# Loading half of the first memory features first, and moving their transposes and three copies, in the head of a gated cross attention kernel

## The chip, the cores and the metric

The kernel runs on one core of a Trainium2 chip. Its metric is the device time of one execution in microseconds (us). All data are float32. The engines are called as the profile calls them: PE is TensorE (with PEld, its weight loads), DVE is VectorE, ACT is ScalarE, POOL is GpSimd, and SP issues most of the DMAs. SBUF is the on-chip memory of 128 partitions, PSUM the accumulators that PE writes.

## The reference

It is cross attention to a short memory, with a gate and a norm. Batch 8, 1024 tokens of 1024 features, 64 memory rows of 512 features for each batch entry:

```python
memory_proj = einsum('bme,de->bmd', memory, W_mem)               # (8, 64, 1024)
scores = einsum('bnd,bmd->bnm', hidden_states, memory_proj) / sqrt(D)
attn = softmax(scores, axis=-1)
memory_context = einsum('bnm,bmd->bnd', attn, memory_proj)
gate_input = concatenate([hidden_states, memory_context], axis=-1)
gate = sigmoid(einsum('bnf,df->bnd', gate_input, W_gate) + b_gate)
fused = hidden_states + gate * memory_context
return fused * rsqrt(mean(square(fused), axis=-1) + 1e-6) * norm_w
```

The host hands the kernel W_mem and W_gate transposed, so that their rows are features of the input.

## The kernel before, in words

The main loop takes the 8192 tokens in 16 groups of 512. The large product (tokens by the upper half of W_gate) is made by two nested levels of a scheme with seven products in the place of eight; sums of operands run on DVE and POOL, sums of results mostly on DVE. Ahead of the loop stands a setup of some 80 us: the projected memory (products `pm1` to `pm7`), then its product with the lower half of W_gate (`mg1` to `mg7`, rows `pg` of the profile), and the sums of the W_gate blocks that the loop uses. This change touches only the first microseconds of that setup, the head.

All instructions of the head are pinned: each engine runs its own in the order in which the program writes them, and each waits by semaphores for what it reads or overwrites. There is no planner at work there.

The head, in the order of the program. Line numbers are those of the profile of before.

1. `zeros` is cleared (L115), and PE runs four warm-up matmuls `pz` on it. A float32 matmul shows as two records in the profile, a transpose as one.
2. SP issues the loads (L98), 512 KB each: the first half of the memory (`memq[0]`: 256 of the 512 memory rows, two to a partition, with all 512 features), chunks 0 and 1 of W_mem (`wm[:, k]`, a chunk being 128 input features by 1024 outputs), the second half of the memory (`memq[1]`), chunks 2 and 3. The eight chunks `w2` of the lower half of W_gate, two loads of 2 MB of the upper half (`w1`) and the norm's weights follow at once on the same queue.
3. `transpose_mem(0)` (L193): PE turns the first half of the memory, one 128x128 block at a time. For each chunk k of 128 features it makes two transposes into the PSUM tile `pt[k]`, and a copy (L200) brings the result into `memT` in SBUF. Even k is copied by DVE, odd k by ACT. `memT[0]` holds k = 0 and 1, `memT[1]` holds k = 2 and 3.
4. The products read halves of W_mem's columns that lie interleaved; some are copied first into dense tiles. `pw[:, 0]` is such a copy of chunk 1 (POOL, L284), `pw[:, 1]` of chunk 2 (ACT, L285), `pw_b[:, 0]` of chunk 3 (ACT, L290), `pw22` of the other halves of chunks 2 and 3 (ACT, L298).
5. Product 1 (`p1`): its first half takes chunk 0 straight from `wm` and k = 0 of `memT`, its second half `pw[:, 0]` and k = 1. Each half is 8 matmul records.
6. DVE makes `ps1` in two halves, sums of chunk 0 with chunk 2, and of chunk 1 with chunk 3 (L95, `pm_s<-wm` 128x512).
7. `transpose_mem(1)` does the same for the second half of the memory; here k = 0, 1 are copied by ACT, k = 2, 3 by DVE. It writes other columns of the same four PSUM tiles.
8. ACT copies product 1's result to `pu` (L293).
9. Product 2 reads the columns of `memT[1]` (k = 2, 3) that belong to the first half of the memory: first half `pw[:, 1]`, second half `pw_b[:, 0]`, 8 records each.
10. DVE makes `pt1`, `ps2`, `pt2`; product 5 needs `ps1` and `pt1`, product 6 `ps2` and `pt2`. DVE adds product 2 to `pu` and goes on with `ps3` and `ps4`; POOL makes two sums `e12` (after `pt1`) and `e21` (after `pt2`), in place in `memT`. Product 7 needs `ps3` and `e12`, product 3 `ps4`, product 4 `pw22` and `e21`. POOL then starts the sums `t1`, `t2` (rows `t_w`) of the `w2` chunks; `t2` is needed by the product `mg6`.

Of the kernel before, what the change touches and what calls it, by code (L numbers as in the profile page):

```python
# [10 lines left out]
ALU = mybir.AluOpType  # L11
# [9 lines left out]
def tile_gated_cross_attention_rmsnorm(  # L21
# [42 lines left out]
    nc = tc.nc  # L64
    B, N, D = x.shape
    M, E = mem.shape[1:]
# [5 lines left out]
    KE = E // P  # L72
# [16 lines left out]
    pin = tc.keep_in_program_order  # L89

    def mm(o, lhsT, rhs, start, stop):
        pin(nc.tensor.matmul(o, lhsT, rhs, start=start, stop=stop, skip_group_check=True))  # L92

    def tt(eng, o, a, b, op):
        pin(eng.tensor_tensor(o, a, b, op))  # L95

    def load(o, i):
        pin(nc.sync.dma_start(o, i))  # L98

    def t4k(pool, shape, tag, name):  # L100
        return pool.tile(shape, F32, tag=tag, name=name)
# [9 lines left out]
    def bank(tag, shape, name):  # L111
        return ps.tile(shape, F32, tag=tag, name=name)
# [1 line left out]
    zeros = t4k(small, [P, C], "junk", "zeros")  # L114
    pin(nc.vector.memset(zeros, 0.0))  # L115
    pz = bank("af0", [P, C], "pz")
    for _ in range(4):
        mm(pz, zeros[:, :P], zeros, True, True)


    memr = mem.rearrange("b m e -> (b m) e").rearrange("(g p s) e -> g p s e", g=2, p=P)
    memq = [t4k(rot, [P, 2, E], "l2", f"memq{i}") for i in range(2)]
    wm = t4k(xqpool, [P, KE, D], "xq", "wm")
    wmr = w_mem_t.rearrange("(k p) d -> p k d", p=P)
    load(memq[0], memr[0])
    for k in (0, 1):
        load(wm[:, k, :], wmr[:, k, :])
    load(memq[1], memr[1])
    for k in (2, 3):
        load(wm[:, k, :], wmr[:, k, :])  # L130
# [51 lines left out]
    mgd = dram.tile([2, BM, D], F32, name="mgd")  # L182
    memT = [t4k(rot, [P, 2, BM], "u", f"memT{i}") for i in range(2)]

    def transpose_mem(g):


        cols = slice(g * (BM // 2), (g + 1) * (BM // 2))
        for k in range(KE):
            for r in range(2):  # L190
                n = 2 * g + r
                pin(
                    nc.tensor.transpose(  # L193
                        pt[k][:, n * P : (n + 1) * P], memq[g][:, r, k * P : (k + 1) * P], ident
                    )
                )
            o = memT[k // 2][:, k % 2, cols]
            copy = nc.scalar.copy if (k < 2 if g else k % 2) else nc.vector.tensor_copy
            pin(
                copy(  # L200
                    o.rearrange("p (c r) -> p r c", r=2),
                    pt[k][:, cols].rearrange("p (r c) -> p r c", r=2),
                )
            )
# [33 lines left out]
    def split(t, r):  # L238

        return t.rearrange("p k (m j) -> p k j m", j=KD)[:, :, KH * r : KH * (r + 1), :]  # L240

    def pm_left(pool, tag, name):
        return t4k(pool, [P, 2, KH, P], tag, name)

    def pm_product(n, l, r, k_first=False):

        pgs = [setup_bank(f"pm{n}_{i}") for i in range(2)]
        if not isinstance(l, tuple):
            l = l[:, 0], l[:, 1]
        order = [(j, k) for j in range(KH) for k in range(2)]  # L250
        if k_first:
            order.sort(key=lambda jk: jk[1])
        for j, k in order:
            o = pgs[j // 2][:, (j % 2) * HM : (j % 2 + 1) * HM]
            mm(o, l[k][:, j, :], r[:, k, :], j % 2 == 0 and k == 0, k == 1)
        return pgs
# [7 lines left out]
    w11, w12 = (split(wm[:, 2 * k : 2 * k + 2, :], 0) for k in range(2))  # L264
    w21, w22 = (split(wm[:, 2 * k : 2 * k + 2, :], 1) for k in range(2))
# [5 lines left out]
    ps1 = pm_left(apool, "s1", "pm_s1")  # L271
# [6 lines left out]
    def pm_dense(o):  # L278
        t = const.tile([P, 3, 2, C], F32, tag=f"it{o}", name=f"pm_it{o}")[:, :2]
        return t.rearrange("p a k c -> p (a k c)").rearrange("p (k j m) -> p k j m", k=2, j=KH)  # L280

    pw22, pw, pw_b = pm_dense(1), pm_dense(2), pm_dense(3)
    transpose_mem(0)
    pin(nc.gpsimd.tensor_copy(pw[:, 0], w11[:, 1]))  # L284
    pin(nc.scalar.copy(pw[:, 1], w12[:, 0]))  # L285
    p1 = pm_product(1, (w11[:, 0], pw[:, 0]), e11, True)
    for k in range(2):
        tt(nc.vector, ps1[:, k], w21[:, k], w22[:, k], ALU.add)
    transpose_mem(1)
    pin(nc.scalar.copy(pw_b[:, 0], w12[:, 1]))  # L290
    for i in range(2):
        pin(
            nc.scalar.copy(  # L293
# [733 lines left out]
```

## Time and profile before

| | |
|---|---|
| median of 3 runs | 953.75 us (953.73, 953.75, 954.67) |
| the profiled execution | 953.63 us |
| its span, first to last instruction | 951.8 us |
| PE busy | 939.9 us, 99% of the span |
| DVE, POOL, ACT busy | 806.5, 711.0, 361.9 us |
| from PE's first matmul to the first transpose | 1.19 to 4.76 us |
| transposes of the first half of the memory | 4.76 to 6.47 us |
| product 1 | 6.47 to 10.17 us |
| transposes of the second half | 10.17 to 11.04 us |
| product 2 | 11.04 to 14.50 us |

A row of the timeline begins with its start and its length in us; then come the engine, the line, the operation, the output tile and the tiles that it is made from, shapes, and how many records it merges. The bracket at the end, where there is one, is the time for which the engine stood idle before it, and what ended that. In the digit rows of the page each digit is one fortieth of the span, some 24 us, and 9 means 90% busy or more. The chain of work that ended last is followed backwards from the last instruction, at each step to what released it. Names come without buffer numbers: `pm_it` stands for `pw`, `pw_b`, `pw22`, `pt1`, `pt2` and `ps4`, `pm_s` for `ps1` to `ps3`, `pm_t` for `pu`.

### The profile page before, as it was taken

The numbers are of one execution on the slowest core, as the hardware profiler recorded it, in microseconds if no ns is written. First come the engines' busy times: TensorE is split into PE (matmuls) and PEld (weight loads), VectorE is DVE, ScalarE is ACT, GpSimd is POOL, SyncE is SP. The second block draws the span as 40 slices with busy tenths as digits, with TensorE's granted clock in tenths as the row PEclk, the third lists the DMA queues.
The fourth block names the chain that finished last, engine by engine and source line by source line (L and its number), as shares of the span: only waits on it lengthen the run. The fifth ranks groups of instructions, "written<-read, shape, count | busy, mean of one in ns | idle before, by whom it ended". The sixth has DMA issues, their size and how long they took to land.

```text
span 951.8 us, 15584 instructions
## 1 busy us (share of the span) xinstructions
PE 939.9 (99%) x5624; PEld 732.1 (77%) x5624; DVE 806.5 (85%) x1258; ACT 361.9 (38%) x782; POOL 711.0 (75%) x780
## 2 busy tenths in 40 slices
PE   9999999999999999999999999999999999999995
PEld 8546778787877778787877778687877778787773
DVE  6988888888888888888888888888888888888887
ACT  3001235162433525153443526253443526243456
POOL 5997877688676777787686867777686767877683
PEclk9999999999999999999999999999999999999998
DMA  9956664482919365481918366391918466390632
GB/s 377 285 144 161 105 122 112 108 181 48 206 46 185 98 130 131 103 185 39 217 45 174 93 141 138 90 199 32 215 53 166 101 133 144 79 210 25 144 142 89
DMA packets 70923, 128.40 MB, mean 135 GB/s; under 512 B 12352, under 2 KB 49216, under 8 KB 70592
## 3 DMA queue, kind: packets, MB, share of 16 engines
q1 hardware_dynamic: 61664, 93.86, 37.5%
q0 software_dynamic: 9184, 33.56, 19.4%
q8 instruction: 45, 0.74, 0.3%
q14 instruction: 30, 0.25, 0.1%
HBM read 87.56 MB, written 41.68 MB: 136 GB/s over the span
## 4 chain that ended last, share of the span: by engine, by line
PE 97%; DVE 2%; ACT 1%; issue 0%; DVEq 0%
PE af L92 31%; PE ed L92 21%; PE pc L92 10%; PE kC L92 10%; PE kB L92 10%; PE pg L92 5%; PE psT_af L92 5%; PE pm L92 3%; DVE gate L95 1%; PE psT_ed L92 0%; PE pz L92 0%; DVE gate L788 0%; PE sc L430 0%; PE pa L461 0%; PE psT_b L92 0%; PE pt L193 0%
## 5 line engine op out<-in xcount | busy, mean ns | idle before, releaser
L95 POOL TENSOR_TENSOR gate<-gate,u 128x512 f32<-128x512 f32 (+1 forms) x224 | 236.9, 1070 | 187.4 <-DVE u L95 151.3
L685 ACT ACTIVATE gate<-gate 128x512 f32<-128x512 f32 x128 | 80.2, 630 | 225.0 <-DVE gate L95 225.0
L352 DVE STREAM_TRANSPOSE a<-xq 128x512 f32<-128x512 f32 x128 | 141.5, 1108 | 3.4 <-issue 3.4
L95 POOL TENSOR_TENSOR l<-a 128x256 f32<-128x256 f32 x128 | 110.9, 866 | 18.6 <-PE af L92 17.5
L714 DVE SCALAR_TENSOR_TENSOR gate<-gate,ss,nw_sb 128x512 f32<-128x512 f32 x120 | 119.4, 995 | 1.1
L92 PE MATMUL pc<-mg,attnT 64*64 64x512 f32 x512 | 116.8, 595 | 0.1
L92 PE MATMUL ed<-it,l 128*128 128x256 f32 x448 | 115.0, 379 | 0.0
L92 PE MATMUL kB<-it,l 128*128 128x256 f32 x448 | 115.0, 379 | 0.0
L95 DVE TENSOR_TENSOR gate<-gate,pc 128x512 f32<-128x512 f32 x128 | 86.1, 682 | 31.7 <-ACT gate L685 31.7
L901 ACT COPY u<-af 128x256 f32<-128x256 f32 x112 | 40.7, 363 | 182.6 <-PE af L92 182.6
L92 PE MATMUL af<-w,a 128*128 128x256 f32 x384 | 98.5, 379 | 0.0
L92 PEld LDWEIGHTS kB<-it,l 128*128 128x128 f32 x448 | 85.1, 190 | 11.6
L95 DVE TENSOR_TENSOR gate<-gate,ed 128x512 f32<-128x512 f32 x112 | 76.1, 679 | 19.1 <-POOL gate L95 17.5
L92 PEld LDWEIGHTS ed<-it,l 128*128 128x128 f32 x448 | 83.9, 190 | 10.7
L95 DVE TENSOR_TENSOR gate<-gate,af 128x512 f32<-128x512 f32 (+1 forms) x128 | 76.7, 609 | 12.8 <-PE af L92 11.2
L92 PEld LDWEIGHTS af<-w,a 128*128 128x128 f32 x384 | 73.0, 190 | 10.3 <-issue 0.5
L95 POOL TENSOR_TENSOR l<-s 128x256 f32<-128x256 f32 x96 | 78.2, 814 | 3.3 <-DVE it L95 3.3
L92 PEld LDWEIGHTS pc<-mg,attnT 64*64 64x64 f32 x512 | 32.9, 132 | 50.1 <-issue 23.5
L92 PE MATMUL af<-mg,attnT 64*64 64x256 f32 (+1 forms) x384 | 67.4, 456 | 0.0
L92 PE MATMUL ed<-it,a 128*128 128x256 f32 x256 | 67.4, 386 | 0.0
L95 DVE TENSOR_TENSOR u<-u,kC 128x256 f32<-128x256 f32 x112 | 45.9, 410 | 23.8 <-PE kC L92 20.3
L92 PE MATMUL af<-t,s 128*128 128x256 f32 x256 | 65.8, 379 | 0.0
(147 smaller groups left out, 2044.6 us busy)
## 6 DMA issues: line engine op xcount, KB each, us to landing
xq<-in_x SPq DMA_DIRECT2D x64, 512.0 KB, 10.3
gate<-in_x POOLq DMA_DIRECT2D x60, 512.0 KB, 8.4
out<-gate SPq DMA_DIRECT2D x60, 512.0 KB, 3.3
w<-in_w_gate_t SPq DMA_DIRECT2D x8, 512.0 KB, 10.2
w<-in_w_gate_t SPq DMA_DIRECT2D x2, 2048.0 KB, 17.2
mg<-mgd SPq DMA_DIRECT2D x16, 256.0 KB, 5.2
wm<-in_w_mem_t SPq DMA_DIRECT2D x4, 512.0 KB, 6.0
mpd<-mpT SPq DMA_DIRECT2D x4, 512.0 KB, 8.6
```

Source lines behind the costliest of these rows:

```text
L92: pin(nc.tensor.matmul(o, lhsT, rhs, start=start, stop=stop, skip_group_check=True))
L95: pin(eng.tensor_tensor(o, a, b, op))
L352: nc.vector.transpose(A[key][:, :, r * P : (r + 1) * P], chunks(xq[q][:, 4 * t : 4 * t + 4, :], KD)[:, half * KH : (half + 1) * KH],)
L685: pin(nc.scalar.activation(g, g, AF.Sigmoid))
L714: nc.vector.scalar_tensor_tensor(g[:, cols], g[:, cols], rstd[:, t % 2 : t % 2 + 1], nw_sb[:, cols], ALU.mult, ALU.mult,)
L901: pin(nc.scalar.copy(p1, af[:, 0]))
```

## The change

Four edits, all in the head:

- One of the four warm-up matmuls is left out.
- The first half of the memory is loaded in two pieces: features 0 to 255 (k = 0, 1) in front, features 256 to 511 (k = 2, 3) behind chunks 0 and 1 of W_mem. Each piece has 256 KB, in runs of 1 KB where the whole load had runs of 4 KB.
- Only k = 0 and 1 are transposed ahead of product 1; k = 2 and 3 are transposed behind it, just ahead of the second half of the memory. In the first half k = 0 is now copied by DVE and k = 1, 2, 3 by ACT (before: 0 and 2 by DVE, 1 and 3 by ACT).
- The copies of chunks 2 and 3 (`pw[:, 1]`, `pw_b[:, 0]`) go from ACT to POOL, which runs them behind its copy of chunk 1; that of chunk 3 keeps its place in the program behind the transposes of the second half. DVE makes the second half of `ps1` behind its two copies of the second half's transposes, no longer ahead of them.

```diff
-    for _ in range(4):
+    for _ in range(3):
         mm(pz, zeros[:, :P], zeros, True, True)
...
-    load(memq[0], memr[0])
+    load(memq[0][:, :, : E // 2], memr[0][:, :, : E // 2])
     for k in (0, 1):
         load(wm[:, k, :], wmr[:, k, :])
+    load(memq[0][:, :, E // 2 :], memr[0][:, :, E // 2 :])
     load(memq[1], memr[1])
...
-    def transpose_mem(g):
+    def transpose_mem(g, ks=range(KE)):
         cols = slice(g * (BM // 2), (g + 1) * (BM // 2))
-        for k in range(KE):
+        for k in ks:
...
-            copy = nc.scalar.copy if (k < 2 if g else k % 2) else nc.vector.tensor_copy
+            copy = nc.scalar.copy if (k < 2 if g else k) else nc.vector.tensor_copy
...
-    transpose_mem(0)
+    transpose_mem(0, range(2))
     pin(nc.gpsimd.tensor_copy(pw[:, 0], w11[:, 1]))
-    pin(nc.scalar.copy(pw[:, 1], w12[:, 0]))
+    pin(nc.gpsimd.tensor_copy(pw[:, 1], w12[:, 0]))
     p1 = pm_product(1, (w11[:, 0], pw[:, 0]), e11, True)
-    for k in range(2):
-        tt(nc.vector, ps1[:, k], w21[:, k], w22[:, k], ALU.add)
+    transpose_mem(0, range(2, KE))
+    tt(nc.vector, ps1[:, 0], w21[:, 0], w22[:, 0], ALU.add)
     transpose_mem(1)
-    pin(nc.scalar.copy(pw_b[:, 0], w12[:, 1]))
+    tt(nc.vector, ps1[:, 1], w21[:, 1], w22[:, 1], ALU.add)
+    pin(nc.gpsimd.tensor_copy(pw_b[:, 0], w12[:, 1]))
```

## The prediction

> **What bounds the kernel now.** I read the shares of the engines first, then the chain of work that ended last cut to the start, then the timeline of the first 17 us engine by engine. The page's first rows:
>
> ```profile
> PE   9999999999999999999999999999999999999995
> ...
> PE 97%; DVE 2%; ACT 1%; issue 0%; DVEq 0%
> ```
>
> TensorE is busy in every slice but the last. The waits list has one wait of PE, 1.2 us for the zeros at the start; its last matmul starts at 940.85 and a fixed tail of sums, roots and stores follows. So whatever the head saves or loses reaches the end one for one, unless a later stage turns it into a wait. The chain over the first 30 us:
>
> ```profile
> 1.19 3.78 PE pz L92 x8
> 4.97 1.71 PE pt L193 x8
> 6.67 3.66 PE pm L92 x16
> 10.33 0.87 PE pt L193 x8
> 11.21 19.00 PE pm L92 x88
> ```
>
> The head is warm-up matmuls, transposes of the first half of the memory (T0), product 1, transposes of the second half (T1), products 2, 5, 6 and so on, back to back. By start times: T0 4.76, product 1 at 6.47, its second half at 8.44, T1 10.17, product 2 at 11.04, product 5 at 14.50. The same transposes take 1.71 us first and 0.87 later. Looked at in windows of 0.1 us, a 256-column matmul record starts every 0.427 us up to 6.47 and every 0.216 us after that (0.240 where its weights are read straight from W_mem); a transpose record every 0.213, later 0.109. So the clock rises near 6.7, though the clock row prints 9 for that slice too.
>
> The other engines around the two chunks of W_mem that come late:
>
> ```profile
> 6.85 1.11 POOL L284 COPY pm_it<-wm 128x512 f32<-128x512 f32 x1 [5.55 <-DMA wm<-in_w_mem_t]
> ...
> 9.38 1.13 ACT L285 COPY pm_it<-wm 128x512 f32<-128x512 f32 x1 [2.27 <-DMA wm<-in_w_mem_t]
> 9.46 1.10 DVE L95 TENSOR_TENSOR pm_s<-wm 128x512 f32<-128x512 f32 x1 [2.75 <-DMA wm<-in_w_mem_t]
> ...
> 10.74 1.12 DVE L95 TENSOR_TENSOR pm_s<-wm 128x512 f32<-128x512 f32 x1 [0.18 <-DMA wm<-in_w_mem_t]
> ...
> 11.14 1.14 ACT L290 COPY pm_it<-wm 128x512 f32<-128x512 f32 x1
> ```
>
> These name the landings: chunk 1 at 6.80, chunk 2 at 9.36, chunk 3 at 10.64; with issue plus landing time of the DMA view, memory half 0 at 4.24, chunk 0 at 5.48, memory half 1 at 8.10. One 512 KB load lands every 1.28 us, so loading is a line in fixed order at about 410 GB/s. Product 2 needs chunk 2's copy (10.51) and, for its second half at 12.77, chunk 3's (12.28): 0.5 us of slack each.
>
> **What the skill says.** "SBUF — State Buffer", Who interferes with whom: GpSimd shares its SBUF port with VectorE; a VectorE instruction with two SBUF inputs and a GpSimd instruction that reads SBUF exclude each other for a whole instruction, and the first to issue gets the port. The trace agrees:
>
> ```profile
> 13.01 2.05 DVE L95 TENSOR_TENSOR pm_s<-pm_s,wm 128x1024 f32<-128x1024 f32 x1
> ...
> 13.20 3.59 POOL L95 TENSOR_TENSOR memT<-memT,memT 128x512 f32<-128x512 f32 x1 [5.23 <-DVE pm_it L95]
> ```
>
> POOL's 128x512 sum takes 1.26 us alone; here it waits out ps2 (13.01) and pt2 (14.95, 0.71) and takes 3.59, and the next takes 5.03 behind two more such sums. "TensorE: Matmul & The Clock Gate", Part 1: the array runs at half clock until a busy window of about 3.4 us has passed, and the window is free-running. The trace has the half rate, ended 5.5 us after PE's start; that its phase varies from run to run no single trace shows. Part 4 says that transposes don't count as busy in the same way; here the clock rose with half of the last 3.4 us spent in transposes.
>
> **The change, part by part.** My clock for it: full rate from 6.7, as before.
>
> *One warm-up fewer* (two records): PE is free at 4.76 - 2 x 0.427 = 3.91. The half-width load brings 256 KB: 4.24 - 0.64 = 3.60. It moves 1 KB pieces instead of 4 KB; in the packet records a 4 KB packet takes 159 ns and a 1 KB one 46 at its quickest (loads of x and small stores, later), so each half costs 4 x 46 / 159 = 1.16 of its share, +0.1 us. It lands at 3.7, hidden by the warm-ups. If 1 KB packets cost 80 ns, as the median while loads and stores mix, it is +0.6 us for each half; I take 0.1. From here chunk 0 lands at 4.94, chunk 1 at 6.26, the other features of half 0 at 7.0, memory half 1 at 8.3, chunks 2 and 3 at 9.56 and 10.84, 0.2 later than before. One more issue on SP (0.4 us) is hidden: issues run ahead of the data.
>
> *T0 halved*: 4 records, 3.91 to 4.77. Product 1's first half needs chunk 0 and the DVE copy of k=0 (5.43 - 0.85 = 4.58, to 5.01); weights after 4.94+0.05, matmul at 5.2: a new gap of 0.4 us. Then 3.5 records up to 6.7 and 4.5 x 0.24: 7.75. Second half: POOL's copy of chunk 1 runs 6.31 to 7.43, so it is in time; 8 x 0.216 gives 9.48. Before: 10.17. That is 0.7 us ahead.
>
> *The moved transposes*, four records at full rate: 0.43 us, so 9.92. T1 follows, but its k=2 and k=3 write tiles that ACT is still reading: ACT copies k=2 from 9.89 (0.40) and k=3 to about 10.6. T1 ends at 10.86 rather than 10.79. Product 2 could start 0.18 us ahead of before.
>
> *Copies of chunks 2 and 3 from ACT to POOL.* This is where I see the gain go. POOL's copy of chunk 2 and DVE's first half of ps1 wait for the same landing. POOL starts 0.05 us after its landing (6.80, 6.85), DVE 0.10 (9.36, 9.46; 10.64, 10.74). So POOL gets the port: copy 9.61 to 10.73, product 2 at 10.86. DVE's add goes 10.73 to 11.83 instead of 9.66. POOL's copy of chunk 3 is called at 10.89, waits for that add, and runs 11.83 to 12.95 (DVE's two copies then read PSUM). Product 2's second half is due at 10.86 + 1.73 = 12.58 and starts at 13.0. DVE: the second half of ps1, now behind its copies, reaches the port at 12.6, waits, 12.95 to 14.05; pt1 0.70, 14.75. Product 5 needs it: 14.78, PE itself being ready at 14.72. Before: 14.50. Sum: **+0.28 us**.
>
> *Behind that*: ps2 (2.05) and pt2 (0.71) end at 17.4, product 6 due 18.23. POOL's e12 ends about 18.7, product 7 due 21.7. ps3 and ps4 end near 22.8, product 3 due 25.1. POOL's e21 ends near 24, two us later than 21.79; its next deadline is t2 for the second-stage product at 38.2, finished at 34.6 before: 3.6 us of cover, then priced at nothing. At 81.96 POOL idles 3.29 us and the lag ends. ACT only loses work.
>
> The profiled run took 953.63 us (span 951.8, 1.83 around it), 0.12 below the median of 953.75. 953.63 + 0.28 = **953.9**.
>
> **The rivals.**
> *Gain kept*: the small load costs nothing and copy and add don't block each other. Product 2 at 10.86, no further wait, product 5 at 14.31: -0.2, 953.4. For it: the trace has no POOL copy beside a DVE add. Against it: 13.20.
> *Slower: DVE takes the port first at chunk 2's landing.* Then add 9.66 to 10.76, POOL's copy to 11.88, product 2's first half 11.9 to 13.65. DVE's second half of ps1 arrives at 11.53, while the copy holds the port, and gets it before POOL's next copy. Precedent:
>
> ```profile
> 26.67 7.97 POOL L95 TENSOR_TENSOR t_w<-w,t_w 128x512 f32<-128x512 f32 x4
> ...
> 27.35 2.73 DVE L95 TENSOR_TENSOR t<-w 128x2048 f32<-128x2048 f32 x1 [0.41 <-DMA w<-in_w_gate_t]
> ```
>
> where the waiting sum went ahead of POOL's second sum (3.3 us). Then ps1, pt1, ps2, pt2 follow with no pause (1.10 + 0.70 + 2.05 + 0.71): 16.3; chunk 3's copy ends at 17.4, product 5 starts at 19.2: +4.7, 958.3 (up to 960 if PE's wait of 3.8 us drops its clock). It decides as soon as POOL's lead is lost. Against it: at 931.38 an idle POOL and an idle DVE, released together, started 26 ns apart; POOL, ahead, took its plain 1.26 and DVE 1.79 instead of 0.74. For it: at 86.06 POOL led by 19 ns and lost (1.29 instead of 0.73). My lead is 50 ns.
> *Clock late*: the gap of 0.4 us, or the phase, puts the rise one window (3.4 us) later. Product 1 ends at 11.07, T1 12.45, product 5 at 15.9: +1.4, 955.0. Against it: the trace's rise came with transposes in the window, and the new gap is shorter than the transposes that leave it.
>
> **The numbers.** Near 953.9: 0.70. Gain kept: 0.10. DVE first: 0.13. Clock late: 0.07. A difference under 0.2%, 1.9 us, can't be told from none here. Same: 0.70 + 0.10 + 0.07 = 0.87, less 0.01 for a lucky clock that I give to faster, 0.86; slower 0.13. Range 953.0 to 955.6: gain kept with an early clock at the lower end (one run of before was 0.9 above the others, so I allow as much for phase), late clock and dearer 1 KB packets at the upper; DVE first stays outside.
>
> **What would show it.** Right: T0's four records at 3.9 us; a gap of PE near 5; POOL copy of chunk 2 at its plain 1.1 us and DVE's first add about 2.2 us beside it; POOL's copy of chunk 3 about 2 us long; PE waiting 0.4 us inside product 2; product 5 within 14.5 to 14.9. Wrong: POOL's copy of chunk 2 longer than 2 us and a PE gap of 4 us before 17; the half rate lasting past 8; the first memory load landing after 3.9; or product 5 before 14.4.

## The result, and the profile after

The changed kernel takes 955.69 us (median of 22 runs, 954.45 to 957.11), the kernel before 953.74, measured beside it (22 runs, 953.32 to 955.86). The ratio is 1.0021, with a 95% interval of 1.0015 to 1.0027: slower by 1.95 us, where the prediction had 953.9 and a range up to 955.6. The 22 times stand in two clusters with nothing between: twelve from 954.45 to 955.74 and ten from 956.37 to 957.11. A single profiled execution can't show both.

The profiled execution took 954.45 us, the fastest of all, with a span of 952.5. PE is still busy in every slice but the last (99% of the span). The waits of PE in the first 80 us (each line: total us, times, longest):

```profile
PE pz L92 <- DVE zeros L115: 1.2, 1, 1.2
PE pm L92 <- POOL pm_it L285: 0.4, 1, 0.4
PE pm L92 <- DMA wm<-in_w_mem_t: 0.2, 1, 0.2
```

Before, the wait for the zeros was the only one. Now PE waits twice more, once for chunk 0 and once for POOL's copy of chunk 1. The chain that ended last, cut to the first 40 us, names what lies behind that second wait:

```profile
2.10 5.22 DMA wm<-in_w_mem_t
7.33 0.05 issue
7.38 1.11 POOL pm_it L285
8.49 0.04 issue
8.53 1.99 PE pm L92 x8
10.53 1.43 PE pt L194 x12
11.95 21.08 PE pm L92 x96
33.03 7.30 PE pg L92 x17
```

The chain of before was PE back to the warm-ups. This one leaves PE at 8.53 and goes through POOL's copy to a landing at 7.33: chunk 1 of W_mem now sets the start of product 1's second half. Behind that half stand twelve transposes, 1.43 us, where the chain of before had eight, 0.87. The timeline of the same stretch:

```profile
4.07 1.09 PE L194 MATMUL pt<-ident,memq 128*128 128x128 f32 x4
...
5.39 2.73 PE L92 MATMUL pm<-memT,wm 128*128 128x256 f32 x8 [0.23 <-DMA wm<-in_w_mem_t]
7.38 1.10 POOL L285 COPY pm_it<-wm 128x512 f32<-128x512 f32 x1 [6.08 <-DMA wm<-in_w_mem_t]
...
8.53 1.99 PE L92 MATMUL pm<-memT,pm_it 128*128 128x256 f32 x8 [0.41 <-POOL pm_it L285]
...
10.36 1.59 PE L194 MATMUL pt<-ident,memq 128*128 128x128 f32 x12
10.62 1.14 POOL L286 COPY pm_it<-wm 128x512 f32<-128x512 f32 x1 [2.14 <-DMA wm<-in_w_mem_t]
10.67 2.05 DVE L95 TENSOR_TENSOR pm_s<-wm 128x512 f32<-128x512 f32 x1 [5.48 <-DMA wm<-in_w_mem_t]
...
11.91 1.80 POOL L292 COPY pm_it<-wm 128x512 f32<-128x512 f32 x1 [0.15 <-DMA wm<-in_w_mem_t]
...
15.60 6.64 PE L92 MATMUL pm<-pm_it,pm_s 128*128 128x256 f32 x30
```

PE starts its transposes 0.7 us earlier than before, and product 1 1.1 us earlier. Product 1's second half starts 0.09 us later than before (8.53 against 8.44), product 5 1.10 later (15.60 against 14.50), and PE's last matmul 1.11 later (941.96 against 940.85): what is lost by product 5 reaches the end one for one in this execution. From the second half to product 5 the stretch grew from 6.06 to 7.07 us. By start times, that is 0.58 for the transposes, 0.23 and 0.10 for the halves of product 2, and 0.10 for the half of product 1 itself. The first record of each of these three halves stands behind a wait for a copy and takes 0.320 us and not 0.216; the other 0.12 us is PE's wait for the 1.80 us copy of chunk 3, ahead of the second half of product 2.

The loads, by stretches of 2 us (the columns after the window's length are the busy time of PE, PEld, DVE, ACT and POOL, the granted clock, the DMA share and GB/s). Before:

```profile
2.00:4.00 2.00, 2.00 (x6) 1.55 (x6) 0.00 (x0) 0.02 (x1) 0.00 (x0) 1.00 0.91 332
4.00:6.00 2.00, 2.00 (x9) 1.71 (x8) 0.43 (x1) 0.14 (x1) 0.00 (x0) 1.00 1.03 403
6.00:8.00 2.00, 2.00 (x11) 2.00 (x10) 0.42 (x1) 0.65 (x2) 1.11 (x1) 1.00 1.02 412
```

After:

```profile
2.00:4.00 2.00, 2.00 (x5) 1.12 (x4) 0.00 (x0) 0.02 (x1) 0.00 (x0) 1.00 0.79 250
4.00:6.00 2.00, 1.77 (x7) 1.29 (x7) 0.43 (x1) 0.39 (x1) 0.00 (x0) 1.00 0.99 336
6.00:8.00 2.00, 2.00 (x8) 1.67 (x6) 0.00 (x0) 0.00 (x0) 0.62 (x1) 1.00 0.97 336
```

From 2.0 to 8.0 us the changed kernel moved 2 x (250 + 336 + 336) = 1844 KB, the one before 2294. The 450 KB between them are 1.1 us at 410 GB/s, and chunk 2, needed by product 2, lands at 10.57 and not at 9.36. The other traced executions, described below, say the same: over the first 8 us the ten that load the first half whole move 271 to 291 GB/s, the eight with the split of the changed kernel 218 to 248.

### The profile page after: what moved, and what is told of

The parts are those of the page before. It is cut to its first block, busy times and chain, and to the rows that moved or that the text cites. A ratio compares the mean times of both kernels' runs of the same rounds, so it can differ in the third digit from the quotient of the medians.

```text
span 952.5 us, 15581 instructions
## 1 busy us (share of the span) xinstructions
PE 940.4 (99%) x5622; PEld 730.9 (77%) x5622; DVE 807.4 (85%) x1257; ACT 359.9 (38%) x781; POOL 715.0 (75%) x782
## 4 chain that ended last, share of the span: by engine, by line
PE 96%; DVE 2%; ACT 1%; DMA 1%; issue 0%; SPq 0%; POOL 0%; DVEq 0%
PE af L92 31%; PE ed L92 21%; PE pc L92 10%; PE kC L92 10%; PE kB L92 10%; PE pg L92 5%; PE psT_af L92 5%; PE pm L92 2%; DVE gate L95 1%; DMA wm<-in_w_mem_t 1%; PE psT_ed L92 0%; DVE gate L790 0%; PE pa L463 0%; PE sc L432 0%; PE psT_b L92 0%; ACT junk L757 0%
## 5 line engine op out<-in xcount | busy, mean ns | idle before, releaser
L95 POOL TENSOR_TENSOR l<-a 128x256 f32<-128x256 f32 x128 | 113.5, 887 | 18.7 <-PE af L92 17.4
```

## The experiments

The runs were made in groups on several chips, each beside runs of the kernel before (medians 954.11, 953.99 and 954.29 us), and every ratio below is to the runs of its own group. Three numbers describe a head. Chunk 1 is *complete* 0.05 us before POOL's copy of it starts. The half of product 1 that needs it starts 1.20 us after that (0.05, the copy of 1.10, 0.05) unless PE is later. Then product 5. All traced executions:

| kernel | chunk 1 complete | second half of product 1 | product 5 | from half to product 5 | product 5 to last matmul | time |
|---|---|---|---|---|---|---|
| before, four executions | 6.80, 6.98, 8.01, 6.86 | 8.44, 8.20, 9.21, 8.45 | 14.50, 14.36, 15.37, 14.51 | 6.06 to 6.16 | 926.4, 926.5, 926.6, 926.4 | 953.63, 953.76, 954.90, 953.83 |
| changed, six | 7.33, 8.06, 7.73, 8.44, 7.68, 8.35 | 8.53, 9.27, 8.93, 9.64, 8.87, 9.55 | 15.60, 16.71, 16.00, 16.73, 15.91, 16.63 | 7.03 to 7.09; 7.45 | 926.4 five times; 928.1 | 954.45, 955.69, 955.03, 955.54, 954.74, 957.21 |
| changed, whole load, three | 7.84, 7.18, 7.81 | 9.04, 8.38, 9.40 | 15.77, 15.11, 16.02 | 6.62 to 6.73 | 926.4, 926.4, 926.5 | 955.14, 954.53, 955.46 |
| POOL copies alone | 6.86 | 8.06 | 14.44 | 6.37 | 928.1 | 955.44 |
| order alone | 7.84 | 9.03 | 15.88 | 6.84 | 926.4 | 955.13 |
| before, three warm-ups | 7.35 | 8.56 | 14.72 | 6.16 | 926.5 | 954.09 |
| changed, four warm-ups | 7.71 | 8.93 | 16.11 | 7.19 | 926.4 | 955.13 |
| before, load split by features | 9.43 | 10.64 | 16.80 | 6.16 | 926.4 | 955.65 |
| before, load split by rows | 8.95 | 10.16 | 16.32 | 6.16 | 927.3 | 956.12 |
| changed, second half split too | 6.73 | 7.94 | 15.32 | 7.38 | 927.0 | 954.77 |

**The parts of the change, each undone or done alone.** First the changed kernel with its first memory load whole again:

```diff
-    load(memq[0][:, :, : E // 2], memr[0][:, :, : E // 2])
+    load(memq[0], memr[0])
...
-    load(memq[0][:, :, E // 2 :], memr[0][:, :, E // 2 :])
```

> The changed kernel with the first half of the memory loaded whole, in front, in runs of 4 KB; the rest as changed. If the two loads of 1 KB runs are what delays the chunks of W_mem (they landed at 5.25, 7.33, 10.57 and 11.86 us against 5.48, 6.80, 9.36 and 10.64 before), chunks 1 to 3 land within 0.1 us of before, PE's wait for chunk 1's copy goes, product 5 starts at 14.4 to 14.8 instead of 15.60, and the time falls by 0.8 to 1.2 us against the changed kernel. If the copies on POOL or the missing warm-up are the cause, the time falls by less than 0.4 us.

Measured: 954.66 us (13 runs, 954.35 to 956.4), ratio to before 1.0009 (1.0001 to 1.0017). About half of the loss goes, going by the ratios (1.0009 and 1.0021), whose intervals just overlap. The fall is of the size expected, the landings are not: chunk 1 came at 7.84 us in this trace, not near 6.80, and PE still waits for its copy. With the whole load chunks 2 and 3 come earlier (chunk 2 at 9.74 to 10.41 in its three traces, 10.57 to 11.70 in the changed kernel's), and some 0.35 us of the stretch up to product 5 vanish: in the trace POOL's copy of chunk 3 is in time and PE no longer waits for it.

Then, on the kernel before, only the copies and the sum moved:

```diff
-    pin(nc.scalar.copy(pw[:, 1], w12[:, 0]))
+    pin(nc.gpsimd.tensor_copy(pw[:, 1], w12[:, 0]))
...
-    for k in range(2):
-        tt(nc.vector, ps1[:, k], w21[:, k], w22[:, k], ALU.add)
+    tt(nc.vector, ps1[:, 0], w21[:, 0], w22[:, 0], ALU.add)
     transpose_mem(1)
-    pin(nc.scalar.copy(pw_b[:, 0], w12[:, 1]))
+    tt(nc.vector, ps1[:, 1], w21[:, 1], w22[:, 1], ALU.add)
+    pin(nc.gpsimd.tensor_copy(pw_b[:, 0], w12[:, 1]))
```

> The kernel before with one part alone: the copies of chunks 2 and 3 on POOL, and the second half of ps1 behind the second half's transposes, as changed. If the loads are the cause of the loss, this costs little: POOL takes its port first at chunk 2's landing, product 2 starts at 11.0, its second half waits for chunk 3's copy until about 12.8, product 5 starts at 14.5 to 14.7, time +0.0 to +0.3 us against before. If the shared port is the cause, product 5 starts at 15.5 or later and the time is 1 us or more above before; in runs in which DVE takes the port first 4 us or more.

Measured: 954.61 us (13 runs, 953.77 to 956.18), ratio 1.0005 (0.9997 to 1.0013), not told apart from no change. Its trace, 955.44, is of one of its longer executions, and the loss was not in the head: product 5 starts at 14.44, as before. PE's timeline near 70 us, first before:

```profile
66.10 7.03 PE L92 MATMUL pg<-w,mpT 128*128 128x512 f32 x16
```

With the copies on POOL:

```profile
68.23 1.12 PE L92 MATMUL pg<-w,mpT 128*128 128x512 f32 x2 [0.27 <-DVE w L95]
69.91 4.56 PE L92 MATMUL pg<-w,mpT 128*128 128x512 f32 x10 [0.55 <-DVE w L95]
```

PE goes through its queue, finds DVE's four sums `w<-w,t_w` (for the product `mg4`) not ready, and loses 1.7 us against the kernel before: the wait itself and the slower records around it. It is a second place without cover, which no step of the prediction named. In the head the edit costs about half of what the prediction gave it (0.46, from 0.18 ahead to 0.28 behind): from half to product 5 it takes 6.37 us, 0.2 to 0.3 more than before.

The changed kernel with its fourth warm-up back:

```diff
-    for _ in range(3):
+    for _ in range(4):
```

> The changed kernel with the fourth warm-up matmul put back. If the loads are the cause, nothing moves by more than 0.2 us: product 1 waits for chunk 0 and k=0 in any case, and its second half for chunk 1's copy. If the clock rises later in unprofiled runs because PE has less to do early, the median falls by 0.5 to 1.2 us against the changed kernel and its spread (954.45 to 957.11) narrows.

Measured: 955.48 us (13 runs), ratio 1.0015 (1.0007 to 1.0023). Nothing is regained, and nothing lost: PE's start does not matter when chunk 1 sets the pace.

The warm-up removed alone from the kernel before (the reverse of that line):

> The kernel before with one part alone: three warm-up matmuls. The transposes start at about 4.3 us, when the memory lands (4.24), instead of 4.76, and product 5 0.1 to 0.4 us earlier than 14.50 if the clock rises by 6.7. If what the head gains reaches the end, PE's last matmul starts that much before 940.85; if a later stage takes it back (in the second trace of before product 5 came 0.14 us early and the last matmul at the same 940.85), it stays at 940.8 to 940.9. Either way the time is within 0.5 us of before, unless a late clock (half rate beyond 8 us) costs about 1.4.

Measured: 954.29 us (12 runs, 953.39 to 954.76), ratio 0.9998 (0.9989 to 1.0006). An earlier PE gives nothing in the old order either.

The order alone: one warm-up fewer and the moved transposes, with the whole load, the copies of chunks 2 and 3 on ACT and `ps1` as before (k = 2 is copied by ACT, as in the changed kernel):

```diff
-    transpose_mem(0)
+    transpose_mem(0, range(2))
     pin(nc.gpsimd.tensor_copy(pw[:, 0], w11[:, 1]))
     pin(nc.scalar.copy(pw[:, 1], w12[:, 0]))
     p1 = pm_product(1, (w11[:, 0], pw[:, 0]), e11, True)
+    transpose_mem(0, range(2, KE))
```

> The changed kernel with the loads and the copies of chunks 2 and 3 as before: what is left is three warm-ups and the later transposes of k=2, 3. If the loads and the copies on POOL make the loss, the time is within 0.5 us of before and 0.3 to 0.7 us under the run with the whole load: product 2 starts at 11.2 to 11.5, since ACT's copies of k=2, 3 now stand behind its copy of chunk 2, product 5 at 14.7 to 15.0. If the new order itself costs (product 1 meets the landings with no slack, or the clock rises later), the time stays 0.7 us or more above before.

Measured: 955.16 us (13 runs, 954.89 to 956.06), ratio 1.0011 (1.0003 to 1.0019). Its waits of PE:

```profile
PE pm L92 <- POOL pm_it L284: 1.1, 1, 1.1
PE pm L92 <- DMA wm<-in_w_mem_t: 0.6, 1, 0.6
```

PE stands for 1.7 us around product 1 and then makes the four transposes that the kernel before made while these loads were under way. From product 1's second half to product 5 it takes 6.84 us and not 6.06 to 6.16, so moving the transposes costs 0.7 by itself: 0.44 for the four records and 0.25 for pauses between the last four transposes of the second half, whose PSUM tiles ACT empties late here, behind its copy of chunk 2 (0.14 in the changed kernel).

**The load by itself.** The kernel before with the split, both pieces in front, first by features (runs of 1 KB), then by rows (runs of 2 KB):

```diff
-    load(memq[0], memr[0])
+    load(memq[0][:, :, : E // 2], memr[0][:, :, : E // 2])
+    load(memq[0][:, :, E // 2 :], memr[0][:, :, E // 2 :])
```

> The kernel before with one part alone: the first half of the memory in two loads of 256 KB with runs of 1 KB, one behind the other, both in front. If runs of 1 KB are the cause, the second piece lands 0.6 to 1.2 us later than the whole load did (4.24), chunks 1 to 3 land 0.7 to 1.2 us later than before, the first transposes of k=2 wait, product 2 starts 0.5 to 1.2 us later than 11.04 and the time is 0.6 to 1.2 us above before. If they aren't, chunk 2 lands by 9.7 and the time stays within 0.3 us of before.

```diff
-    load(memq[0], memr[0])
+    for r in range(2):
+        load(memq[0][:, r, :], memr[0][:, r, :])
```

> The kernel before with the first half of the memory in two loads of 256 KB, both in front, as in the run with the split by features, but split by rows: runs of 2 KB, 128 pieces in each load instead of 256. If it is the number of pieces of a load (SP needed 0.68 us to issue 256 of them, 0.39 for 128; data began to flow at 2.2 us instead of 1.77, and the next load's first packets took up to 0.95 us), issues take about 0.4 us, chunk 1's first engine lands by 6.7 (7.06 with the split by features, 6.43 before), chunk 2's by 9.3 (9.96, 8.99), and the time is within 0.6 us of before, at least 1 us under the split by features. If it is the second load as such, or the shorter run, the loss is like that of the split by features: 1.5 to 2.5 us.

Measured: by features 956.11 us (7 runs), ratio 1.0025 (1.0014 to 1.0037); by rows 955.31 (21 runs), 1.0013 (1.0006 to 1.0020). Both were misses: I expected 0.6 to 1.2 us of the first and got 2.0, and 0.6 at most of pieces of 2 KB and got 1.3. The three longest executions by features (957.0 to 958.7) and four of the longer ones by rows (956.05 to 956.6) have a mean granted clock of PE of 0.994, the others 0.996 to 0.998, so part of these figures may be the clock, and the intervals of the two splits overlap. In both traces the head behind chunk 1 is untouched, 6.16 us from half to product 5; what the head loses lies ahead of it. (By rows another 0.9 us is lost behind product 5; more on that below.) Split by features, a load of 256 pieces takes SP 0.68 us to issue, against 0.39 for 128 pieces of 4 KB, and data flows from 2.2 us and not from 1.77. By rows the issue (0.39) and the first data (1.76) are as before, so the issue alone doesn't explain the loss. Chunk 1 at 9.43 and 8.95 is also late for another reason: by the trace's records of landings, the first of the 16 DMA engines had its share of chunk 1 in by 7.06 and 6.55, and the slowest came 2.4 us later.

The changed kernel with the second half of the memory split in the same way:

> The changed kernel with the second half of the memory split too, into two loads of 256 KB with runs of 1 KB, in its old place. If loads of 1 KB runs delay what stands behind them, chunk 2's first engine lands 0.4 to 0.9 us later than in the changed kernel (8.78 for the memory's second half, 10.06 for chunk 2), product 2 starts that much later, and the time rises by 0.4 to 0.9 us against the changed kernel. If they don't, product 2 stays at 11.8 and the time within 0.3 us.

Measured: 955.95 us (15 runs), ratio 1.0022 (1.0014 to 1.0029), no different from the changed kernel. A miss: I had chunk 2 later, and it landed at 10.31.

**Is it chance between executions?** Both kernels traced again, with no edit.

> The changed kernel once more, for a second trace. If the spread of its times comes from the slowest of the 16 DMA engines (in the trace at hand chunk 1's sixteen landings span 6.24 to 7.33 us), the landings of chunk 1 and the start of product 1's second half (8.53) move together by some tenths to 1.5 us, and product 5 with them. If it comes from the clock, the half rate ends at another time than 6.75 us after the start.

> The kernel before once more, for a second trace. If its steps have half a microsecond of slack to the loads (memory 4.24 against 4.76, chunk 1's copy 7.97 against 8.44, chunk 2's 10.51 against 11.04), product 5 starts at 14.5 again within 0.1 us as long as the slowest engine is late by less than that. If its landings are late by more, product 5 is late by the excess.

> The changed kernel once more, for a third trace. From the two at hand: product 5 starts at 15.60 with the clock up at 6.75 and chunk 1 landed at 7.33, at 16.71 with 10.75 and 8.06; before 14.50 and 14.36. If both terms are at work, a clock that rises by 7.5 us gives product 5 at 15.2 to 16.2, depending on chunk 1's last landing, and one beyond 9 us 0.7 to 1.4 us more.

> The changed kernel a fourth time, for the same reason and with the same expectation: product 5 at 15.2 to 16.2 us where the clock rises by 7.5 us, 0.7 to 1.4 more where it rises beyond 9, and PE's last matmul later than before's 940.85 by the same amount as product 5 is later than 14.50, or by up to 1.3 more where DVE's sums at 62 to 68 us are late.

Measured, in the order of these four (the table has them): product 5 at 16.71, 14.36, 16.00 and 16.73 us. It follows chunk 1 (8.06, 6.98, 7.73, 8.44) in the changed kernel, and the clock besides, whose rise lies at 10.75 in the first of these executions and at 4.24 in the last. The last is a miss: with an early clock I had product 5 by 16.2.

The next four ask whether the pieces of 1 KB make chunk 1 late: the kernel with the whole load twice, the kernel before twice.

> The changed kernel with the first half of the memory loaded whole, as in the earlier run of the same kernel; one more look at when chunk 1 of W_mem is complete. If the pieces of 1 KB make chunk 1 late (landings of 7.33 to 8.44 us in four traces of the changed kernel), it is complete by 7.1 here, like the three traces of 6.80 to 6.98 with the whole load and four warm-ups, product 1's second half starts by 8.4 and product 5 by 15.5. If the whole load comes just as late once PE starts its transposes earlier (7.34, 7.83 and 7.84 in the three traces with the whole load and three warm-ups), it is complete after 7.3 again, and the pieces are not the cause.

> The kernel before, once more, for the spread of its landings. If its landings are early by its own making, chunk 1 is complete at 6.8 to 7.0 again and product 5 starts near 14.4. If the earlier ones were luck, it is complete anywhere from 6.8 to 7.9, as in the traces with three warm-ups; product 5 then starts up to 15.2.

> As the run of this kernel just before it: complete by 7.1 if the pieces are the cause of the late chunk 1, after 7.3 if not. With the earlier one this makes three traces of the whole load against four of the split one.

> As the third look at the kernel before: chunk 1 complete at 6.8 to 7.0, or anywhere from 6.8 to 7.9 if the earlier ones were luck.

Measured: the whole load in the changed order had chunk 1 at 7.18 and 7.81, between the two expectations and then at the later one, and the kernel before once at 8.01, later than I allowed and with no edit at all, against 6.80 to 6.98 in its other three. In that late execution the chain of before reads like that of after:

```profile
1.65 6.36 DMA wm<-in_w_mem_t
8.01 0.05 issue
8.06 1.11 POOL pm_it L284
...
9.21 1.99 PE pm L92 x8
```

It took 954.90 us. So the landing of a load varies by 1.2 us between executions of one program. What moves is its slowest DMA engine: the first of the 16 had its share of chunk 1 at 6.12 to 6.46 us in every kernel whose first load was whole or had only its first half in front, and the last 0.4 to 2.0 us later. The lag was 0.4 to 1.6 us (mean 1.0 of ten executions) with whole loads, 0.6 to 2.0 (mean 1.5 of eight) with the changed kernel's split. The means point to the pieces, but the ranges overlap. The number of warm-ups does as well: with whole loads chunk 1 was complete at 7.18 to 7.84 in all five traces with three, and by 6.98 in four of the five with four. Single packets explain some of it: in the late execution of before two packets of 4 KB took 1.06 and 1.11 us near 5.5 us, where the median is 0.159; but the third whole load in the changed order had as long a lag with none over 0.45. What makes one engine late stays open.

**The upper cluster.** The changed kernel traced twice more, for an execution above 956.4 us:

> The changed kernel once more. Of its 22 measured times 10 lie between 956.4 and 957.1 us, above all four of its traced executions (954.45 to 955.69). If chunk 1 alone sets the time, product 1's second half starts 1.2 us after chunk 1 is complete, product 5 7.07 to 7.1 later (7.44 with a late clock), and an execution near 956.7 has chunk 1 complete near 9.4, or near 9 with the clock rising late. If something else adds to it, product 5 starts before 17.5 us in an execution above 956.4, and PE waits later.

> As the run just before it: the time follows the completion of chunk 1 (plus 1.2, plus 7.07 to 7.44 to product 5), or an execution above 956.4 us shows a wait of PE behind product 5.

The second is one, 957.21 us. Its chunk 1 (8.35) and product 5 (16.63) are no later than in the execution of 955.54; PE's last matmul is. Its waits of PE have a line that the first of the two (954.74 us) lacks:

```profile
PE pg L92 <- DVE w L95: 0.8, 2, 0.5
```

It is the wait of the copies-alone kernel. Where DVE became late shows in the timelines of DVE and POOL behind product 5. The execution of 954.74:

```profile
15.49 2.04 DVE L95 TENSOR_TENSOR pm_s<-pm_s,wm 128x1024 f32<-128x1024 f32 x1
15.69 3.58 POOL L95 TENSOR_TENSOR memT<-memT,memT 128x512 f32<-128x512 f32 x1 [1.67 <-DVE pm_it L95]
17.42 0.71 DVE L95 TENSOR_TENSOR pm_it<-memT,pm_it 128x512 f32<-128x512 f32 x1
...
19.23 5.03 POOL L95 TENSOR_TENSOR memT<-memT,pm_it 128x512 f32<-128x512 f32 x1
```

The execution of 957.21:

```profile
16.22 2.02 DVE L95 TENSOR_TENSOR pm_s<-pm_s,wm 128x1024 f32<-128x1024 f32 x1
16.38 2.99 POOL L95 TENSOR_TENSOR memT<-memT,memT 128x512 f32<-128x512 f32 x1 [1.64 <-DVE pm_it L95]
18.15 1.76 DVE L95 TENSOR_TENSOR pm_it<-memT,pm_it 128x512 f32<-128x512 f32 x1
...
20.07 1.28 POOL L95 TENSOR_TENSOR memT<-memT,pm_it 128x512 f32<-128x512 f32 x1 [0.70 <-DVE pm_it L95]
...
21.30 3.06 POOL L95 TENSOR_TENSOR t_w<-w 128x512 f32<-128x512 f32 x1
23.14 3.02 DVE L95 TENSOR_TENSOR pm_it<-wm,pm_s 128x1024 f32<-128x1024 f32 x1
```

In both, POOL's first sum waits out DVE's `ps2`. In the first DVE's `pt2` goes next (0.71 us, its plain length) and POOL waits on; in the second POOL goes and `pt2` takes 1.76. POOL's second sum then takes 1.28 instead of 5.03, POOL is early with `t_w`, and its sums hold up DVE's `ps3` and `ps4` as well. "SBUF — State Buffer" of the Trainium skill (Who interferes with whom) has that the first to issue blocks the other; here an operation that already waits is sometimes passed by the other engine's next one: of the 20 traces `pt2` went first in eleven and POOL in nine. What decides it the traces don't show. POOL's sum starts 0.161 to 0.175 us behind `ps2` where POOL won; where `pt2` did, 0.156 to 0.160 in three traces and 0.174 to 0.199 in eight.

When POOL wins, DVE works without a pause from there on: it begins its transposes of the projected memory (`mpq`) 28.2 us after the start of `ps2`, in all nine traces. When `pt2` wins, DVE has pauses in which it waits for PE, and `mpq` begins 25.2 to 25.9 us after product 5. So what POOL's win costs depends in part on how far `ps2` starts ahead of product 5. In the order of before that is 1.2 to 1.5 us, `mpq` begins at most 27.0 after product 5, and its executions lose 0.2 us at most by it. With the second half of `ps1` behind POOL's copies it is mostly 0.4, `mpq` begins 27.8 after product 5, and three kernels that were caught so (957.21 us, the copies alone, the second half split too) lost 1.7, 1.7 and 0.6. A second thing enters, since the kernel split by rows lost 0.9 with `ps2` 1.2 ahead. From the start of `mpq` to the end of the four sums `w<-w,t_w` it takes 26.3 to 26.6 us in 17 traces and 27.7 in three (957.21, the copies alone, the split by rows), in which the four sums themselves take 6.27 us and not 4.8 to 5.8. The two together give the loss: the sums end 55.4 us behind product 5 where 1.7 was lost (twice), 54.6 where 0.9, 54.3 where 0.6, and 53.6 at most in the other sixteen traces, which lost 0.2 at most. Why the four sums are longer in three of the nine is open. How it reaches PE is in the chain of the 957.21 us execution:

```profile
41.72 7.14 DMA xq<-in_x
...
65.86 6.20 DVE w L95 x4
...
72.11 7.99 PE pg L92 x18
```

The load of x stands on SP behind the last store that waits for DVE, so it is issued 2.2 us later than in the execution of 955.54 (39.55); DVE's work on x and its sums follow, and end at 72.05. Only this one execution of the changed kernel was traced above 956.4 us; that the ten times of the upper cluster have the same cause is likely, but not shown.

## Why the prediction was wrong, step by step

**One warm-up fewer, and the load: the step that failed first.** PE started its transposes at 3.9 to 4.1 (3.9 predicted), and the first piece of the memory landed at 3.78 to 3.94 against 3.7. But the step had chunk 1 at 6.26 and chunk 2 at 9.56. Measured: 7.33 to 8.44, and 10.57 to 11.70. Two terms were wrong in size. The cut load was priced by its packets alone, +0.1 us for each half, and its issue was called hidden; it cost 1.1 us of loading by 8.0 us in the profiled execution. The packets kept their price: the 512 of 1 KB take 46 ns in the median and 55 in the mean there. The loss lies outside them, in what the sum left out. The issue of the first load stands ahead of all data and took 0.68 us instead of 0.39, data flowed 0.44 us later, and after that the rate was 336 GB/s instead of 403 to 412, with single packets of 4 KB of up to 0.86 us; how the loss divides among these stays open. So the dearer case of 80 ns a packet, +0.6 for each half, has the size of the loss by luck. And a landing was read from one trace as a fixed time, where it has a spread of 1.2 us in the kernel before.

**The order.** The gap near 5, 0.4 us in the prediction, came as 0.2 to 1.0. The step had product 1's second half at 7.75, with chunk 1's copy in time: it starts at 8.53 to 9.64. Thus the 0.7 us that PE was ahead was spent waiting, and the transposes that moved behind chunk 1 were paid after the wait. Before, PE had 0.4 us of slack to chunk 1; the change turned it into a wait and put 0.7 us more work behind it (order alone 6.84, before 6.06 to 6.16). The length itself was right: 0.43 us for the four and 0.94 for T1 make 1.37, and they took 1.45; wrong was that an earlier product 1 would pay for them.

**Copies of chunks 2 and 3 to POOL: right in kind, too large in size.** POOL took the port 0.05 us ahead of DVE in every trace of it, kept its plain 1.1, DVE's add took 2.05 (2.2 predicted), the copy of chunk 3 1.80 (2 predicted), and PE waited inside product 2 for it, 0.12 us and not 0.4 in the profiled execution. The whole step was some 1 us later in time there, since chunk 2 was. The rival in which DVE goes first, to which the prediction gave its 0.13 for slower, never came at this place. Most of the signs that were to show the prediction right stand around this step, and most of them came while the time was wrong; none stood at the landing of chunk 1.

**Behind that: priced at nothing, and that was the second failure.** The step looked at POOL's lag and its cover of 3.6 us up to `t2`. It took from one trace that POOL loses the port behind `ps2`. In nine of 20 traces POOL wins, and then it can be DVE that has no cover at 70 us: 1.7 us in the trace of 957.21. The middles of the two clusters of times (956.8 and 955.4) are 1.4 apart.

**Clock late.** PE ran at half rate beyond 8 us in two of the six traces. In one the rise was at 10.75, inside product 1's second half, and product 5 came 7.45 after the half of product 1 rather than 7.03 to 7.09, +0.4 us. In the other, that of 957.21, it fell between 8.8 and 9.55, ahead of that half, where PE had to wait for chunk 1's copy until 9.55 in any case. "TensorE: Matmul & The Clock Gate" of the Trainium skill (Part 1) calls the window free-running, and these traces agree: the rise lay anywhere from 4.24 to 10.75 us with the same program. It explains no large part of the loss.

**The sum.** Over the six traces against the four of before, by means: the second half of product 1 comes 9.13 - 8.58 = 0.55 us later, the stretch to product 5 takes 7.13 - 6.11 = 1.0 longer, and the way to the last matmul 0.2 longer with the port lost in one of six. That is 1.8; the medians differ by 1.95. The share of the port would be larger if the ten of 22 runs in the upper cluster lose it, which is not shown.

No version that was tried beats the kernel before; one warm-up fewer and the copies alone can't be told from it.

## What to carry to other kernels

Work that PE does while it would otherwise wait for a load costs nothing; moved behind the wait, it is paid in full (0.7 us here). So before putting work later ask what PE will do at its old place and which transfer ends last there. Cutting a load in two has a price that its packets don't show, so measure it by the next loads' landings. Take landings from several executions and as the last of the 16 DMA engines: a slack of 0.4 us to a load is none where that load varies by more than 1 us. And where two engines share a port, look at who would suffer under either winner, far behind the change too: one trace shows one winner.

## What the runs showed of the hardware

- The 16 shares of one load don't land together: the last of chunk 1 came 0.4 to 2.4 us after the first, and with the program of before anywhere from 0.4 to 1.6.
- As the first load of the program, one of 256 pieces of 1 KB held SP for 0.68 us and its data began to flow at 2.2 us, one of 128 pieces of 4 KB for 0.39 with data from 1.77. In the profiled execution after, packets of 1 KB took 46 ns in the median, packets of 4 KB 159.
- Of two engines that wanted the shared port, the one that was already waiting (POOL) was passed by the other's next sum in eleven of 20 traces.
- With PE starting at 1.19 us in all 20 traces, its clock had risen by 4.42 us in one and rose at 10.75 in another; in one execution it rose amid the first four transposes (4.24), so they did not keep it from rising.
- The first 256-column matmul after a wait takes 0.320 us to the start of the next, where those behind it take 0.216 (with the clock risen).
